# Cross-attention with two levels of Strassen products on one core: three sums of the next A move to the second stage, product 4's copied state changes its buffer, and a block's eviction changes its place

## The chip, the cores and the metric

The kernel runs on 1 core of one Trainium2 chip. The metric is the time of one execution in device microseconds (us); a kernel is run several times and the median is compared. The engines are TensorE (PE; its weight loads are a row of their own, PEld), VectorE (DVE), ScalarE (ACT), GpSimd (POOL) and SyncE (SP). SP, ACT and POOL also issue DMAs; those that POOL issues here with `accum_op` add the source to what lies in the destination.

## The reference

For each of 8 batches, with x1 and x2 of 512 x 1024 (channels x positions), in float32:

```python
q = jnp.einsum('bcn,dc->bnd', x1, Wq) + bq          # D = 64
k = jnp.einsum('bcn,dc->bdn', x2, Wk) + bk[:, None]
v = jnp.einsum('bcn,dc->bdn', x2, Wv) + bv[:, None]
attn = jax.nn.softmax(jnp.einsum('bnd,bdm->bnm', q, k), axis=2)
out = jnp.einsum('bcm,bnm->bcn', v, attn) + x1
```

## The kernel before

The kernel doesn't form v. It computes E, the exponentials of the scores with m on the partitions, then in a **first stage** Y = x2 E (512 x 1024, contracted over 1024 positions), whose columns are divided by the sums of E, and in a **second stage** O = Wv Y (contracted over 512 channels). Bias bv and x1 are added when O leaves PSUM.

Both stages are one 2 x 2 Strassen-Winograd step: seven products of blocks instead of eight. The left matrix (A, loaded as the transpose of x2; W in the second stage) gives four sums, the right one (E, then Y) four more:

```python
LEFT = (
    ("S1", "21", "22", ALU.add),
    ("S2", "S1", "11", ALU.subtract),
    ("S3", "11", "21", ALU.subtract),
    ("S4", "12", "S2", ALU.subtract),
)
```

The right sums T1 to T4 are built alike. `sum_a` makes the left sums of A on DVE (line 109, 128x1024 each; S3 overwrites block 21), `sum_e` and `sum_y` the right ones (line 254). `MULT` says which blocks product i multiplies and in which PSUM pair it accumulates: products 1, 6, 5, 3 run one after the other in the pair "a" (a0, a1), products 2, 7, 4 in the pair "c" (c0, c1; 2 by itself, 7 and 4 together). `multiply` issues a whole product (line 301: 16 matmuls in the first stage, 8 in the second), and after products 1, 6 and 5 ACT copies the running state of "a" to SBUF (line 312, tiles u1, u6, u5). These tiles become the place where a result block is put together: `evict_o` adds PSUM and bias to the tile on DVE (line 496), has POOL issue the accumulating DMA of x1 into it (line 499) and SP the store (line 500). Block 12 goes through ACT into a tile of tag "r" (line 492) instead. So block 11 of O is completed in u1, 22 in u5, 21 in u6.

From the second batch on, products 2, 3 and 4 of the first stage are themselves done with a Strassen step (the inner step): `inner_left` (line 333, four 128x256 operations) and `inner_right` (line 344, four 128x512) make its sums on DVE, `inner_product` its seven small products (line 351) with ACT copies between them (line 360). `multiply_2` is product 2; its two chains stand in c0 and c1, and its results are added on DVE (line 397). `multiply_onto` is product 3 (in "a") or 4 (in "c"): ACT copies go to a tile d and a tile v, and `complete` (line 422, DVE) adds v to d. The tags of d and v are arguments; a tile of a tag with one buffer can be written only when the readers of the tile before in that tag are done. Product 3 has its v in tag "r", product 4 in tag "u1", the tag of the tile that product 1 of the second stage copies to next.

`period(s, n, nn, nnn)` is one turn of the loop over the batches: the first and second stage of batch s, mixed with the scores, maxima and exponentials of the next batch n, the queries and keys of nn and a load for nnn. The program is scheduled by hand (`tc.manual_schedule()`): each engine executes its instructions in the order in which the program issues them, and waits at the head of its queue for what the instruction needs. So the place of a line in `period` is its place in the queue of its engine. Lines that will be spoken of:

- first stage, in order: products 1 and 2, `sum_t4`, S4, T3, product 6, scores of n for half 0 and queries of nn, maxima (`fold`, line 211; `highest`, line 215 and POOL's all-reduce, line 220), product 5, exponentials of n (lines 248 on DVE, 249 on ACT), `start_sum` (ACT line 507, then three accumulating DMAs from POOL, line 509), the right sums of product 3, `sum_a(n, "S1", "S2", "S3")`, product 7, `evict_y` of block 22 (line 462), product 3 with its eviction (lines 422, 442), the scaling of three blocks of Y (line 464), scores of n for half 1 (the third pair of scores stands in "a", its copies are line 197, the others' 199) and keys of nn, T1 and T2 of Y, maxima, `total` (line 215, POOL's all-reduce at line 225), product 4 (its sums at lines 422 and 432), block 21 of Y (lines 462, 464);
- second stage: products 1, 6, 2, 5, 7, 3, 4 on PE, with T3, T4, the exponentials of n for half 1 and the evictions of O on DVE between them, and the inner sums of product 2 of the next batch.

In the first batch (b = 0) there are no inner steps, and S1, S2 and S3 of the next A are made in the second stage already, with block 21 of O between them.

Of the kernel before, what the change touches and what calls it, by code (L numbers as in the profile page):

```python
# [15 lines left out]
def kernel(  # L16
# [117 lines left out]
    def sum_a(s, *ks):  # L134
        for k in ks:
            if k != "S3":
                s.a[k] = sb.tile([P, MH, C // 2], F32, tag=f"a{k}", name=f"a{k}_{s.b}")
        left_sums(s.a, *ks)
# [188 lines left out]
    def inner_left(s, i, x, tag):  # L327

        v = {f"{p + 1}{q + 1}": x[:, ts(q, MH // 2), ts(p, P)] for p in range(2) for q in range(2)}
        sums = sb.tile([P, 4, MH // 2, P], F32, tag=tag, name=f"aI{i}_{s.b}")  # L330
        for z, (k, x, y, op) in enumerate(LEFT):
            v[k] = sums[:, z]
            nc.vector.tensor_tensor(v[k], v[x], v[y], op)
        s.inner[i] = v
# [29 lines left out]
    def inner_bank(s, i, z):  # L364
        return ps_s.tile([P, 2, H], F32, tag="sc", name=f"ps_i{i}{z}_{s.b}")[:, 0, left]
# [35 lines left out]
    def multiply_onto(s, i, d_tag, v_tag):  # L401

        b0, b1 = (s.bank[MULT[i][2], j] for j in range(2))
        chain, third = inner_bank(s, i, 0), inner_bank(s, i, 2)
        d = sb.tile([P, 2, 2, H // 2], F32, tag=d_tag, name=f"d{i}_{s.b}")
        v = sb.tile([P, 2, H], F32, tag=v_tag, name=f"v{i}_{s.b}")[:, 0, left]
        for z, ps, opens, *copies in (
            (1, chain, True, d[:, 0, 0, :]),  # L410
            (7, third, True, v),
            (6, chain, False, d[:, 1, 0, :]),
            (2, b0[:, left], False),
            (5, chain, False, d[:, 0, 1, :], d[:, 1, 1, :]),
            (4, b1[:, left], False),
            (3, b0[:, right], False),
        ):
            inner_product(s, i, z, ps, opens, *copies)

        def complete():  # L420
            both = v.unsqueeze(1).to_broadcast([P, 2, H // 2])
            nc.vector.tensor_tensor(d[:, 1], d[:, 1], both, ALU.add)

        return d.rearrange("p j a n -> p j (a n)"), complete

    def multiply_4(s):

        d, complete = multiply_onto(s, 4, "u5", "u1")
        complete()
        for j in range(2):  # L430
            u6 = s.tmp[6][:, j, :]
            nc.vector.tensor_tensor(u6, u6, d[:, j, :], ALU.add)
# [33 lines left out]
    def evict_o(s, k):  # L466


        bank, add = RESULT[k]
        r, h = int(k[0]) - 1, int(k[1]) - 1  # L470

        def at(x):
            return x[s.b, 2 * r * P : 2 * (r + 1) * P, ts(h, H)].rearrange("(t p) n -> p t n", p=P)

        def bias(j):
            return bv_sb[:, 2 * r + j : 2 * r + j + 1]

        if s.b == B - 1:
            o = s.x[:, 2 * r : 2 * r + 2, ts(h, H)]
            for j in range(2):  # L480
                nc.vector.scalar_tensor_tensor(
                    o[:, j, :], s.bank[bank, j], bias(j), o[:, j, :], ALU.add, ALU.add
                )
            for j in range(2):
                if add is not None:
                    nc.vector.tensor_tensor(o[:, j, :], o[:, j, :], s.tmp[add][:, j, :], ALU.add)
                nc.sync.dma_start(out[s.b, ts(2 * r + j, P), ts(h, H)], o[:, j, :])
            return
        if add is None:
            o = sb.tile([P, 2, H], F32, tag="r", name=f"r_{s.b}")  # L490
            for j in range(2):
                nc.scalar.activation(o[:, j, :], s.bank[bank, j], AF.Identity, bias=bias(j))
        else:
            o = s.tmp[add]
            for j in range(2):
                nc.vector.scalar_tensor_tensor(  # L496
                    o[:, j, :], s.bank[bank, j], bias(j), o[:, j, :], ALU.add, ALU.add
                )
        nc.gpsimd.dma_start(o, at(x1), accum_op=ALU.add)  # L499
        nc.sync.dma_start(at(out), o)  # L500
# [107 lines left out]
    def period(s, n, nn, nnn):  # L608

        def first(i):
            multiply(s, "y", i, s.a, s.t, MH)

        def second(i):
            multiply(s, "o", i, w, s.y, 2)

        open_t(s)
        if n is None:
            load_x(s, x1)  # L620
        first(1)
        if s.b == 0:
            head_second(s, n)
        sum_e(s, "T1", "T2")
        if s.b == 0:
            total(s, 0)
        else:
            shares(s, 0)
        if n:
            load_a(n, "11")  # L630
        if s.b == 0:
            first(2)
            evict_y(s, "11", (1,))
            keys(n)
            load_x(nn, x1)
            sum_t4(s)
            sums(s, 1)
            shares(s, 0)
        else:
            evict = multiply_2(s)  # L640
            if s.b > 1:
                sums(s, 1)
            evict()
            sum_t4(s)
            sum_a(s, "S4")
            if s.b == 1:
                sums(s, 1)
        sum_e(s, "T3")
        if n:
            load_a(n, "21", "22")  # L650
        first(6)
        if s.b:
            inner_right(s, 4, s.t["T4"], "eT2")
            inner_left(s, 3, s.a["S4"], "aI3")

        def next_queries():
            queries(nn)
            load_x(nn, x2)

        def next_keys():  # L660
            keys(nn)
            if nnn:
                load_x(nnn, x1)

        if n:
            scores_and(n, 0, "c", next_queries if nn else nothing)
            for i in range(1, MH):
                fold(n, 0, i, "max", ALU.max)
            highest(n, 0)
        shares(s, 1)  # L670
        first(5)
        if n:
            for i in range(MH):
                exponentials(n, 0, i)
            start_sum(n, 0)
        if s.b:
            inner_right(s, 3, s.t["22"], "eT1")
            if n:
                sum_a(n, "S1", "S2", "S3")
        first(7)  # L680
        if s.b > 1:
            inner_left(s, 4, s.a["22"], "a12")
        if s.b:
            evict_y(s, "22", (1,))
            multiply_3(s)()
            for k in ("11", "12", "22"):
                evict_y(s, k, (2,))
        else:
            evict_y(s, "11", (2,))
            evict_y(s, "22")  # L690
            first(3)
            evict_y(s, "12", (1,))
        if s.b == 1:
            inner_left(s, 4, s.a["22"], "a12")
        if n:
            scores_and(n, 1, "a", next_keys if nn else nothing)
        sum_y(s, "T1")
        sum_y(s, "T2")
        if n:
            if s.b == 0:  # L700
                left_sums(w, "S1", "S2", "S3", "S4")
            for i in range(1, MH):
                fold(n, 1, i, "max", ALU.max)
            highest(n, 1)
            if s.b:
                total(n, 0)
        if s.b:
            multiply_4(s)
        else:
            first(4)  # L710
        if n:
            load_a(n, "12")
        evict_y(s, "21")
        second(1)
        sum_y(s, "T3")
        sum_y(s, "T4")
        second(6)
        if n:
            exponentials(n, 1, 0)
            exponentials(n, 1, 1)  # L720
        second(2)
        evict_o(s, "11")
        if s.b == 0:
            total(n, 0)
        second(5)
        if n:
            exponentials(n, 1, 2)
            exponentials(n, 1, 3)
        second(7)
        evict_o(s, "22")  # L730
        if n:
            if s.b:
                inner_left(n, 2, n.a["12"], "aS4")
            else:
                sum_a(n, "S1")
            second(3)
            evict_o(s, "12")
            if s.b:
                inner_right(n, 2, n.e[0][:, 1], "eT4")
            else:  # L740
                sum_a(n, "S2")
            second(4)
            evict_o(s, "21")
            if s.b == 0:
                sum_a(n, "S3")
                inner_left(n, 2, n.a["12"], "aS4")
                inner_right(n, 2, n.e[0][:, 1], "eT4")
        else:
            second(4)
            evict_o(s, "21")  # L750
            second(3)
            evict_o(s, "12")
# [37 lines left out]
```

## Time and profile before

| | |
|---|---|
| Time, median of 3 runs (lowest to highest) | 704.3 us (704.13 to 704.95) |
| Profiled execution: its own time | 704.53 us |
| Profiled execution: span from first to last instruction | 702.8 us |
| Granted TensorE clock over it | 0.999 |
| PE busy | 689.1 us, 2144 matmuls |
| DVE busy | 601.5 us, 730 instructions |
| ACT busy | 251.4 us, 390 instructions |
| POOL busy | 173.6 us, 135 instructions |
| Moved by DMA | 102.72 MB, mean 146 GB/s |

The table's durations are those of one profiled execution. A row of the timeline gives the start in us from the span's beginning, the duration, the engine, the line of the kernel, the operation, output and input, their shapes and how many instructions were merged; in brackets stands the idle time of the engine just before and what ended it. A row of the waits gives who waited for whom: us in total, how often, the longest. Periods of the loop are counted by their batch, 0 to 7; in the profile period 1 starts at 122.52 us, period 2 at 209.02, period 6 at 546.87 and period 7 at 629.05.

### The profile page before, as it was taken

To read this page: it belongs to the slowest core of one execution; us is meant where nothing else is said; L and a number is where in the kernel's file an instruction comes from. 1 tells how busy PE (TensorE), PEld (TensorE's weight loads), DVE (VectorE), ACT (ScalarE), POOL (GpSimd) and SP (SyncE) were. 2 spreads that over 40 slices of the span, in tenths; PEclk is the share of its full clock that TensorE was granted. 3 is DMA by queue.
4 is the path that set the end of the run, shared out by engine and by line. 5 is a ranking of instruction groups with operands and counts; after the bars stand their busy time and mean duration, and the time that the engine had idled before them with its cause. 6 is when DMAs were issued, how large, how long until landed. Compare 5 with 4: busy or idle time off the path is not lost.

```text
span 702.8 us, 6246 instructions
## 1 busy us (share of the span) xinstructions
PE 689.1 (98%) x2144; PEld 346.3 (49%) x2144; DVE 601.5 (86%) x730; ACT 251.4 (36%) x390; POOL 173.6 (25%) x135
## 2 busy tenths in 40 slices
PE   8999999999999999999999999999999999899997
PEld 4333444535545455454654556454554545545563
DVE  0998776989989899798998989889898889989584
ACT  2733424146231543225432344423444136232120
POOL 0124314132423123221142222222231222322000
PEclk9999999999999999999999999999999999999999
DMA  9666375864558454765639467285643824269003
GB/s 331 222 214 233 92 209 94 185 196 81 181 103 232 145 101 155 156 187 150 129 118 185 153 173 187 60 181 159 156 89 63 207 76 76 60 107 268 15 1 120
DMA packets 41248, 102.72 MB, mean 146 GB/s; under 512 B 4608, under 2 KB 4608, under 8 KB 41216
## 3 DMA queue, kind: packets, MB, share of 16 engines
q1 hardware_dynamic: 24256, 70.26, 29.3%
q0 software_dynamic: 15696, 29.96, 25.2%
q10 hardware_dynamic: 1264, 2.10, 0.9%
q8 instruction: 17, 0.28, 0.2%
q14 instruction: 15, 0.12, 0.1%
HBM read 72.62 MB, written 16.81 MB: 127 GB/s over the span
## 4 chain that ended last, share of the span: by engine, by line
PE 80%; DVE 12%; DMA 4%; issue 2%; ACT 1%; SPq 1%; POOL 1%; DVEq 0%; ACTq 0%
PE ps_ya L301 21%; PE ps_oa L301 14%; PE ps_oc L301 12%; PE ps_i L351 11%; PE ps_yc L301 7%; PE ps_s L190 5%; PE ps_q L148 3%; PE ps_k L148 3%; PE ps_ya L351 3%; DVE max L211 2%; PE ps_yc L351 2%; DMA a<-in_x2T_dram 1%; DMA x_in_x_dram<-in_x_dram 1%; DVE y L464 1%; DVE e L248 1%
## 5 line engine op out<-in xcount | busy, mean ns | idle before, releaser
L301 PE MATMUL ps_ya<-eT,aS 128*128 128x512 f32 x256 | 113.1, 595 | 0.0
L312 ACT COPY uy<-ps_ya 128x512 f32<-128x512 f32 x48 | 28.1, 588 | 163.7 <-PE ps_ya L301 157.4
L248 DVE TENSOR_TENSOR e<-e,top 128x1024 f32<-128x1024 f32 x60 | 72.0, 1251 | 15.5 <-POOL top L220 15.5
L301 PEld LDWEIGHTS ps_ya<-eT,aS 128*128 128x128 f32 x256 | 48.0, 190 | 60.9 <-issue 59.4
L249 ACT ACTIVATE e<-e 128x1024 f32<-128x1024 f32 x60 | 61.5, 1054 | 27.9 <-DVE e L248 26.4
L220 POOL PARTITION_ALL_REDUCE top<-max x16 | 32.4, 2026 | 146.2 <-DVE max L215 75.3
L301 PE MATMUL ps_yc<-e,a 128*128 128x512 f32 x144 | 63.4, 593 | 0.0
L225 POOL PARTITION_ALL_REDUCE den<-sum x16 | 56.0, 3497 | 22.8 <-DVE sum L215 17.8
L351 PE MATMUL ps_i<-eI,aI 128*128 128x256 f32 x252 | 60.4, 380 | 1.2 <-ACT sum L507 1.1
L301 PE MATMUL ps_oc<-y,w 128*128 128x512 f32 x128 | 57.7, 593 | 1.3 <-DVE y L464 1.3
L301 PE MATMUL ps_oa<-yT,w_S 128*128 128x512 f32 x128 | 57.6, 593 | 1.2 <-ACT uo L312 1.2
L301 PE MATMUL ps_ya<-e,a 128*128 128x512 f32 x128 | 56.3, 593 | 0.8 <-ACT e L243 0.8
L199 ACT COPY e<-ps_s 128x1024 f32<-128x1024 f32 x47 | 46.7, 1027 | 22.3 <-PE ps_s L190 21.3
L312 ACT COPY uo<-ps_oa 128x512 f32<-128x512 f32 x48 | 27.8, 586 | 74.9 <-PE ps_oa L301 60.5
L496 DVE SCALAR_TENSOR_TENSOR uo<-ps_oc,bv_sb,uo 128x512 f32<-128x512 f32 x42 | 30.9, 747 | 27.3 <-PE ps_oc L301 25.1
L351 PEld LDWEIGHTS ps_i<-eI,aI 128*128 128x128 f32 x252 | 47.2, 190 | 9.1 <-ACT sum L507 1.8
L499 POOL DMA_DIRECT2D uo<-in_x_dram x21 | 25.0, 1189 | 104.0 <-DVE uo L496 98.0
L254 DVE TENSOR_TENSOR eT<-e,eT 128x1024 f32<-128x1024 f32 x32 | 48.8, 1545 | 0.5
L190 PE MATMUL ps_s<-q,k 64*128 64x512 f32 x188 | 47.3, 608 | 1.6 <-ACT q L524 0.8
L509 POOL DMA_DIRECT2D sum<-e x21 | 25.3, 1205 | 78.2 <-DMA sum<-e 58.7
L301 PEld LDWEIGHTS ps_yc<-e,a 128*128 128x128 f32 x144 | 27.3, 190 | 34.8 <-issue 33.6
L211 DVE TENSOR_TENSOR max<-max,e 128x1024 f32<-128x1024 f32 x32 | 39.2, 1225 | 3.7 <-ACT e L197 0.5
(117 smaller groups left out, 1063.7 us busy)
## 6 DMA issues: line engine op xcount, KB each, us to landing
x_in_x_dram<-in_x_dram SPq DMA_DIRECT2D x60, 512.0 KB, 6.0
a<-in_x2T_dram SPq DMA_DIRECT2D x32, 512.0 KB, 6.7
sum<-e POOLq DMA_DIRECT2D x21, 512.0 KB, 5.0
uo<-in_x_dram POOLq DMA_DIRECT2D x21, 512.0 KB, 5.9
out_dram<-uo SPq DMA_DIRECT2D x21, 512.0 KB, 4.5
x_head<-in_x_dram SPq DMA_DIRECT2D x8, 512.0 KB, 8.2
den<-row POOLq DMA_DIRECT2D x16, 256.0 KB, 3.6
r<-in_x_dram POOLq DMA_DIRECT2D x7, 512.0 KB, 6.0
```

Source lines behind the costliest of these rows:

```text
L148: nc.tensor.matmul(ps[r, :], w_sb[:, c, :], s.x[:, c, ts(h, H)], start=(c == 0), stop=(c == CT - 1),)
L190: nc.tensor.matmul(ps[g], s.k[r, ts(i, P)], s.q[r, ts(h, H)], start=True, stop=True)
L199: nc.scalar.copy(e[:, :, i, :], whole)
L211: nc.vector.tensor_tensor(f, e[:, :, 0, :] if i == 1 else f, new, op)
L220: nc.gpsimd.partition_all_reduce(s.top[h], s.mx[h][:, 0, :], P, ReduceOp.max)
L225: nc.gpsimd.partition_all_reduce(s.den[h], s.mx[h][:, 0, :], P, ReduceOp.add)
L248: nc.vector.tensor_tensor(e, e, top, ALU.subtract)
L249: nc.scalar.activation(e, e, AF.Exp)
L254: nc.vector.tensor_tensor(t[k], t[x], t[y], ALU.subtract)
L301: nc.tensor.matmul(ps, left[ka][:, k, ts(j, P)], right[kb][:, k, :], start=opens and k == 0, stop=i in (2, 3, 4) and k == n_k - 1, skip_gr ...
L312: nc.scalar.copy(s.tmp[i][:, j, :], ps)
L351: nc.tensor.matmul(ps, s.inner[i][ka][:, k, :], s.inner[i, "t"][kb][:, k, :], start=opens and k == 0, stop=z in (2, 3, 4) and k == MH // 2 ...
```

## The change

Three edits, all in the order of instructions and in one tag:

1. From the second batch on, S1, S2 and S3 of the next A are no longer made in the first stage (between the right sums of product 3 and product 7), but in the second: S1 and S2 ahead of the eviction of block 22 of O, S3 behind it, ahead of the inner sums of product 2.
2. The copied state v of product 4 takes its tile from tag "r" instead of "u1".
3. In the first batch S1, S2, S3 and the inner sums of the next batch's product 2 all stand ahead of the eviction of block 21 of O, which becomes DVE's last step there. (In later batches block 21 was last before.)

```diff
     def multiply_4(s):
-        d, complete = multiply_onto(s, 4, "u5", "u1")
+        d, complete = multiply_onto(s, 4, "u5", "r")
...
         if s.b:
             inner_right(s, 3, s.t["22"], "eT1")
-            if n:
-                sum_a(n, "S1", "S2", "S3")
         first(7)
...
         second(7)
+        if s.b and n:
+            sum_a(n, "S1", "S2")
         evict_o(s, "22")
         if n:
-            if s.b:
-                inner_left(n, 2, n.a["12"], "aS4")
-            else:
-                sum_a(n, "S1")
+            if s.b == 0:
+                sum_a(n, "S1", "S2")
+            sum_a(n, "S3")
+            inner_left(n, 2, n.a["12"], "aS4")
+            inner_right(n, 2, n.e[0][:, 1], "eT4")
             second(3)
             evict_o(s, "12")
-            if s.b:
-                inner_right(n, 2, n.e[0][:, 1], "eT4")
-            else:
-                sum_a(n, "S2")
             second(4)
             evict_o(s, "21")
-            if s.b == 0:
-                sum_a(n, "S3")
-                inner_left(n, 2, n.a["12"], "aS4")
-                inner_right(n, 2, n.e[0][:, 1], "eT4")
```

The same instructions are issued as before; the queues of PE, POOL and SP and the order on ACT stay as they were.

## The prediction

> **What bounds the kernel now.** I read the page's busy row, then a table of windows with one row for each period of the loop (one batch and the preparation of the next), then the waits, then the timeline of VectorE (DVE) and TensorE (PE) around the places where PE stands still.
>
> ```profile
> PE 689.1 (98%) x2144; PEld 346.3 (49%) x2144; DVE 601.5 (86%) x730; ACT 251.4 (36%) x390; POOL 173.6 (25%) x135
> ...
> 122.52:209.02 86.50, 85.11 (x270) 43.31 (x269) 80.82 (x102) 32.08 (x50) 23.21 (x17) 1.00 0.60 148
> 209.02:293.48 84.46, 84.46 (x270) 43.56 (x269) 75.94 (x93) 31.99 (x50) 22.23 (x17) 1.00 0.61 154
> 293.48:377.94 84.46, 84.46 (x270) 43.56 (x269) 75.90 (x93) 31.98 (x50) 22.27 (x17) 1.00 0.60 153
> ...
> 546.87:629.05 82.18, 78.57 (x237) 41.09 (x237) 75.85 (x93) 29.93 (x47) 22.24 (x17) 1.00 0.44 100
> ```
>
> After the length of the window come the busy times of PE, PEld and DVE. Periods 2 to 5 (four, each 84.46 or 84.47 us) have PE busy from end to end: nothing done to DVE can shorten them. Period 1 takes 86.50, so 2.04 us too much. Period 6 has no projections for a batch after next: two of 3.58 us less, so it should take 84.46 - 7.16 = 77.30; it takes 82.18, 4.9 us too much. With DVE at 75.85 of them, DVE is nearly the bound there. So at most about 6.9 us can be won in the periods whose order changes. The waits say by whom:
>
> ```profile
> PE ps_sa L190 <- DVE y L442: 1.4, 1, 1.4
> PE ps_oc L301 <- DVE y L464: 1.3, 2, 0.8
> PE ps_oa L301 <- ACT uo L312: 1.2, 1, 1.2
> PE ps_i L351 <- ACT sum L507: 1.1, 2, 0.9
> ...
> ACT uo L312 <- DVE d L422: 8.3, 2, 5.0
> ```
>
> Period 6, DVE first, then PE:
>
> ```profile
> 585.61 1.22 DVE L109 TENSOR_TENSOR aS<-a,a 128x1024 f32<-128x1024 f32 x1
> 586.87 1.22 DVE L109 TENSOR_TENSOR aS<-aS,a 128x1024 f32<-128x1024 f32 x1
> 588.01 1.22 DVE L109 TENSOR_TENSOR a<-a,a 128x1024 f32<-128x1024 f32 x1
> 589.14 0.42 DVE L333 TENSOR_TENSOR aI<-a 128x256 f32<-128x256 f32 x1
> ...
> 593.94 1.13 PE L190 MATMUL ps_sa<-q,k 64*128 64x512 f32 x4 [1.36 <-DVE y L442]
> ...
> 607.18 3.70 PE L301 MATMUL ps_oa<-yT,w_S 128*128 128x512 f32 x8 [1.16 <-ACT uo L312]
> 611.65 3.67 PE L301 MATMUL ps_oc<-y,w 128*128 128x512 f32 x8 [0.77 <-DVE y L464]
> ```
>
> The first three rows are S1, S2, S3 of the next A. Everything behind them on DVE's queue, down to block 21 of Y (L464), which product 2 of the second stage needs at 611.65, is late by what they take.
>
> **The change part by part.** The two orders hold the same instructions; TensorE's, SP's and POOL's queues and DMAs are the same. Only DVE's order and one buffer change.
>
> *1. S1 to S3 leave the first stage (periods 1 to 6).* They take 589.14 - 585.61 = 3.53 us of queue. What is late next is no longer DVE: L422 needs ACT's last copy of product 3, L442 its last group on PE. In the undisturbed period 2 these come 1.74 us after that product's group 5 starts (253.24; L422 at 254.98 after an idle of 0.68 for ACT) and 0.82 after its group 3 starts (254.96; L442 at 255.78).
> - Periods 2 to 5: DVE already waited for ACT there. The 3.5 us become waiting: 0.
> - Period 6: group 3 starts at 589.63, so L442 moves from 592.60 to 590.45, 2.15 earlier. Its wait of 1.36 at ps_sa goes (PE gets there at 590.59 + 1.82 = 592.41, L442 is through at 591.7). ACT's copies of the scores are late next: 3.86 us from first to last as in period 1 (171.73 to 175.59), so until 595.63, and product 4 waits some 0.4. PE, 1.46 earlier by then, could start product 2 at 602.43 - 1.46 + 2 x 3.43 = 607.83. From L442 to product 2 DVE takes 611.65 - 592.60 = 19.05, so it starts at 590.45 + 19.05 = 609.50 instead of 611.65: gain 2.15, DVE still the bound.
> - Period 1: group 3 at 169.59 gives L442 at 170.41 instead of 171.09; product 2 at 190.94 instead of 191.62, where PE is ready at about 190.9: gain 0.7. The other 1.05 lost there (PE waits for ACT's sum L507 at 165.20) lies before the moved work and stays.
>
> *2. They come into the second stage.* Period 2's tail, by its own rows:
>
> ```profile
> 281.07 2.34 DVE L248 TENSOR_TENSOR e<-e,top 128x1024 f32<-128x1024 f32 x2
> 285.01 0.75 DVE L496 SCALAR_TENSOR_TENSOR uo<-ps_oc,bv_sb,uo 128x512 f32<-128x512 f32 x1 [1.59 <-PE ps_oc L301]
> 286.72 0.75 DVE L496 SCALAR_TENSOR_TENSOR uo<-ps_oc,bv_sb,uo 128x512 f32<-128x512 f32 x1 [0.96 <-PE ps_oc L301]
> ...
> 291.80 0.75 DVE L496 SCALAR_TENSOR_TENSOR uo<-ps_oc,bv_sb,uo 128x512 f32<-128x512 f32 x1 [0.34 <-PE ps_oc L301]
> 293.52 0.75 DVE L496 SCALAR_TENSOR_TENSOR uo<-ps_oc,bv_sb,uo 128x512 f32<-128x512 f32 x1 [0.97 <-PE ps_oc L301]
> ```
>
> S1 and S2 (2.40) fit into 1.59 + 0.96 of idle: from 283.34 to 285.74, block 22 at 285.74 and, as before, 286.72. S3 (1.14), the inner sums (1.47 and 2.55) then run to about 292.55; block 21 leaves at 292.55 and, as before, 293.52. Zero lag. Behind these evictions wait product 4 (289.9, bank c) and, in the next period, product 2's inner chains in the same bank, 6.87 us after its start: both have over 2 us of slack. In periods 1 and 6 DVE comes later relative to PE (idle only 0.35 before block 22), and ends 0.7 to 0.8 late; the next period's DVE then meets an idle of 0.74 (it waits for ACT's copies at L397), which takes that up. If the cover goes, lag beyond 0.74 passes on to the row maximum, but PE feels it only after a further 2.3 us, by which ACT waits for PE at product 3's first copy. So 0 now, PE time only beyond 3.0 us of lag.
>
> A rule against this: the Trainium skill, SBUF — State Buffer, Who interferes with whom, says that a VectorE instruction with two SBUF inputs and a GpSimd instruction that reads SBUF exclude each other, the second blocking fully. All-reduces run beside L422 and L432 in period 6: 1.53 + 3.33 us there, 0.69 + 1.29 in period 7 without them, 2.88 more. By the row this excess moves along with DVE, since DVE's own maxima and sums release the all-reduces. By the rule, were the issue order to flip, the second L432 would run after the last all-reduce (ends 610.15, plus 0.68, against 609.63): 1.2 us more, period 6 gaining 0.95, the total 1.65. I take the row: periods 1, 2 and 6 all show 3.33.
>
> *3. Product 4's copied state in tag "r".* The two 128x512 copies of product 1 (ACT L312) no longer wait for L422 (5.0 us in period 6), and PE's 1.16 at product 6 goes. But y21 is late behind it, so the wait moves to product 2: 0 on its own. Tag "r" is free: product 3's state is read by 590.3, product 4's is written after 596, block 12 comes 20 us later.
>
> *4. Period 0: block 21 last on DVE.* S3 and the inner sums fill idle of 1.94 + 0.97; block 21 leaves until 125.3 instead of 123.23, and DVE starts T1 about 3 us earlier. But L397 at 134.15 waits for ACT's copy (11.79 after the first product's start, exactly as in period 2): the lead is lost there, gain 0. Cost: block 21's accumulate and store start up to 2.1 later, and ACT's copy of the next product 6 already waits for that store until 140.44. Its second copy is due at 142.34, so up to 1.9 is free; behind it wait four score copies, whose PSUM banks PE needs from 144.91. Bounds: no gain, 0 to 0.3 lost; I take 0, because the accumulate queues behind block 12's anyway (10.3 us to landing).
>
> Sum: 2.15 + 0.7 = 2.85 us. The profiled execution took 704.53 (span 702.8); it would take 701.7. The median shown is 704.3, 0.23 lower: 701.4.
>
> **The rivals.**
> *A, the freed time meets another wait.* In period 6 the sum (L215) needs the third accumulate, issued at 596.57; L215 would be due at 602.18. Landings of 5.0 to 5.8 put it at 601.6 to 602.4. Uncovered, the queue behind it, y21 included, waits. At 7.3 to landing period 6 gains 0.45; with period 1's 0.7 and the price of part 4 the total is about 1.0: 703.3, no change. Likewise with the flipped lock. For it: a margin of 0.6 at the usual 5.0. Against: from 597 to 602 the trace shows no other transfer.
> *B, slower.* The moved sums stretch to double in their new place, beside POOL's issue of block 22's accumulate. Then 3.5 us of lag come in six periods; beyond 3.0, 0.5 to 1.0 us of PE each time, 3 to 6 in all, and periods 1 and 6 keep nothing: 708. It decides at 3.0 us of lag. Against it: aI and eI keep 0.42 and 0.69 right beside that issue (287.77, 1.18 us).
> *C, the change does less than it says:* the buffer is not the product's own but shared with product 3's state and block 12; if one of them were late, ACT would wait as before, which costs nothing while y21 is the bound. Its time is that of the forecast.
>
> **How the numbers follow.** Forecast (with C) 0.80: 701.4, its own range 700.6 to 702.8 (0.8 below for offsets read from other periods, 1.4 above for the same and the lock's 1.2). A 0.12: 703.3. B 0.08: 708. This kernel's time can tell about 0.2%, 1.4 us, from no change. Faster 0.80, same 0.12, slower 0.08. The range goes from 700.6 to 703.9, taking in A and leaving out B.
>
> **What would show it.** Right: windows of periods 2 to 5 unchanged at 84.46, period 6 near 80.0, period 1 near 85.8; no PE wait at ps_sa; ACT's wait for L422 gone; PE's wait at product 2 of period 6 grown to about 1.7, on L464. DVE idle of some 3.5 us before L422 in periods 2 to 5, and next to none before block 22. Wrong: any of the four steady periods longer, S1 to S3 above 1.3 us in their new place, PE waiting for scores in period 1, or L215 waiting for a DMA in period 6.

## The result, and the profile after

The changed kernel takes 701.41 us (median of 5 runs, 701.05 to 701.9) against 704.57 (5 runs, 704.13 to 704.95) on the same chip: ratio 0.9956, 95% interval 0.9942 to 0.9971. A second measurement on another occasion gave 701.31 against 704.24, ratio 0.9958 (0.9946 to 0.9971). The forecast was 701.4. The profiled execution of this kernel took 701.41 us, its span 699.6.

First the page's busy row of the changed kernel, and behind it the windows of periods 1, 2, 3, 6 and 7 (length; busy PE, PEld, DVE, ACT, POOL with counts; granted clock; DMA share; GB/s):

```profile
PE 688.7 (98%) x2144; PEld 346.8 (50%) x2144; DVE 598.7 (86%) x730; ACT 251.4 (36%) x390; POOL 173.7 (25%) x135
...
122.16:207.97 85.81, 84.92 (x270) 43.39 (x269) 77.10 (x97) 32.15 (x50) 23.21 (x17) 1.00 0.58 149
207.97:292.43 84.46, 84.46 (x270) 43.56 (x269) 76.36 (x95) 31.98 (x50) 22.23 (x17) 1.00 0.63 155
292.43:376.89 84.46, 84.46 (x270) 43.56 (x269) 75.22 (x93) 31.98 (x50) 22.27 (x17) 1.00 0.59 153
...
545.81:625.93 80.12, 78.04 (x238) 41.26 (x237) 75.05 (x93) 29.90 (x47) 22.23 (x17) 1.00 0.45 104
625.93:699.60 73.67, 69.64 (x205) 38.42 (x203) 53.86 (x76) 12.05 (x26) 7.29 (x7) 1.00 0.37 103
```

Measured between the first matmuls of product 1, period 1 goes from 86.50 to 85.81 us (0.69 less), periods 2 to 5 take 337.84 both times, and period 6 goes from 82.19 to 80.12 (2.07 less). Period 7 differs by 0.08. The remaining 0.36 us of the spans' 3.2 lies ahead of period 1: before, PE waits twice for 0.2 us on the first loads of x, and among the eleven profiles with the new order of period 0 the start of period 1 lies anywhere from 121.81 to 122.67 us. It is not counted as the change's. So the agreement of 701.41 with the forecast 701.4 to the last digit is in part luck: 0.36 us of the distance did not come from the change.

The rows of the waits that answer to those shown of before:

```profile
PE ps_oc L301 <- DVE y L464: 1.5, 1, 1.5
PE ps_i L351 <- ACT sum L507: 1.1, 2, 0.9
PE ps_i L351 <- ACT e L199: 0.3, 1, 0.3
...
DVE d L422 <- ACT d L360: 26.2, 11, 4.2
```

PE's waits at `ps_sa` for L442 and at `ps_oa` for ACT's copy are gone, and so is ACT's wait for L422. What is left of them stands in one place, product 2 of period 6. The last row is where the time that DVE won in the other periods lies: before L422 it now waits for ACT 11 times, 26.2 us in all, against 9 times and 8.1 us before. Period 6 of the changed kernel, DVE and then PE:

```profile
588.68 0.69 DVE L422 TENSOR_TENSOR d<-d,v 128x512 f32<-128x512 f32 x1 [1.29 <-ACT d L360]
589.47 1.29 DVE L442 TENSOR_TENSOR y<-ps_ya,d 128x512 f32<-128x512 f32 x2
601.21 0.68 DVE L215 TENSOR_TENSOR sum<-sum 128x512 f32<-128x512 f32 x1
603.26 3.33 DVE L432 TENSOR_TENSOR uy<-uy,d 128x512 f32<-128x512 f32 x2
617.04 1.21 DVE L109 TENSOR_TENSOR aS<-a,a 128x1024 f32<-128x1024 f32 x1
618.29 1.23 DVE L109 TENSOR_TENSOR aS<-aS,a 128x1024 f32<-128x1024 f32 x1
620.75 1.22 DVE L109 TENSOR_TENSOR a<-a,a 128x1024 f32<-128x1024 f32 x1
...
594.67 1.99 PE L351 MATMUL ps_i<-eI,aI 128*128 128x256 f32 x8 [0.29 <-ACT e L199]
608.53 3.67 PE L301 MATMUL ps_oc<-y,w 128*128 128x512 f32 x8 [1.55 <-DVE y L464]
```

The rows of L442 and L432 before:

```profile
592.60 1.29 DVE L442 TENSOR_TENSOR y<-ps_ya,d 128x512 f32<-128x512 f32 x2
606.38 3.33 DVE L432 TENSOR_TENSOR uy<-uy,d 128x512 f32<-128x512 f32 x2
```

L422 now waits for ACT, as in the undisturbed periods: the 3.53 us of S1 to S3 no longer stand ahead of it. From L442 to product 2 it is 608.53 - 589.47 = 19.06 us; the prediction took 19.05 from before. L215 starts without idle time, so the third accumulating DMA came in time. L432 still shows 3.33 us for two operations. The last three DVE rows are S1, S2 and S3 in their new place, as long as they were before.

### The profile page after: what moved, and what is told of

It reads as the page before. It is cut to its first block, busy times and chain, and to the rows that moved or that the text cites. A ratio compares the mean times of both kernels' runs of the same rounds, so it can differ in the third digit from the quotient of the medians.

```text
span 699.6 us, 6250 instructions
## 1 busy us (share of the span) xinstructions
PE 688.7 (98%) x2144; PEld 346.8 (50%) x2144; DVE 598.7 (86%) x730; ACT 251.4 (36%) x390; POOL 173.7 (25%) x135
## 4 chain that ended last, share of the span: by engine, by line
PE 86%; DVE 10%; issue 1%; ACT 1%; DMA 1%; POOL 1%; DVEq 0%; ACTq 0%
PE ps_ya L301 21%; PE ps_oa L301 15%; PE ps_i L351 12%; PE ps_oc L301 12%; PE ps_yc L301 8%; PE ps_s L190 5%; PE ps_k L148 4%; PE ps_q L148 3%; PE ps_ya L351 2%; PE ps_yc L351 2%; DVE max L211 2%; DVE e L248 1%; DVE eT L254 1%; DVE e L254 1%; PE ps_sa L190 1%
## 5 line engine op out<-in xcount | busy, mean ns | idle before, releaser
L301 PEld LDWEIGHTS ps_oc<-y,w 128*128 128x128 f32 x128 | 24.1, 190 | 32.8 <-issue 30.6
```

The lines of the kernel that those rows point to most:

```text
L301: nc.tensor.matmul(ps, left[ka][:, k, ts(j, P)], right[kb][:, k, :], start=opens and k == 0, stop=i in (2, 3, 4) and k == n_k - 1, skip_gr ...
```

## The experiments

All kernels of this section were timed against the kernel before on the same chip. Lengths of periods are taken from the profiled execution, as above.

### 1. Each edit by itself

**The moved sums alone**: buffer and first batch as before.

```diff
             inner_right(s, 3, s.t["22"], "eT1")
-            if n:
-                sum_a(n, "S1", "S2", "S3")
...
         second(7)
+        if s.b and n:
+            sum_a(n, "S1", "S2")
         evict_o(s, "22")
         if n:
             if s.b:
+                sum_a(n, "S3")
                 inner_left(n, 2, n.a["12"], "aS4")
```

> Only S1 to S3 of the next A move to the second stage (batches 1 to 7 as n of periods 1 to 6); product 4's state stays in tag u1 and period 0 keeps its old order. Theory (DVE's queue between product 3 and block 21 of Y sets the start of product 2 in periods 1 and 6): the whole gain, 2.8 us against the kernel before; ACT still waits for L422 in period 6 and PE waits about 1.0 at product 6, but product 2 starts when it does in the changed kernel. Rival (the buffer is a cause of its own): only about 1.7 us are won, the 1.16 us of product 6 stay.

Measured: 701.11 us (700.78 to 701.67) against 704.15; ratio 0.9957 (0.9944 to 0.9969). Period 1 takes 85.79, period 6 79.62. The whole gain is this edit's. PE's waits in period 6:

```profile
603.77 3.70 PE L301 MATMUL ps_oa<-yT,w_S 128*128 128x512 f32 x8 [0.50 <-ACT uo L312]
608.24 3.67 PE L301 MATMUL ps_oc<-y,w 128*128 128x512 f32 x8 [0.77 <-DVE y L464]
```

With the old buffer the wait is split, 0.50 at product 6 for ACT's copy and 0.77 at product 2; with the new one (above) it stands whole at product 2, 1.55. The 0.50 was expected as about 1.0. From product 4's second group to product 2 it is 13.85 us here and 13.86 in the changed kernel, so the buffer moves the wait and gains nothing; the 0.5 us by which period 6 is shorter here lies ahead of it (last section).

**The buffer alone** (`multiply_onto(s, 4, "u5", "u1")` becomes `multiply_onto(s, 4, "u5", "r")`, nothing else).

> Only product 4's copied state moves from tag u1 to r. Theory: no change, under 0.1 us; in period 6 PE's wait of 1.16 at product 6 goes and its wait of 0.77 at product 2 grows to about 1.9. Rival (a cause of its own): 1.2 us faster.

Measured: 705.6 us (703.51 to 706.4), ratio 1.0013 (1.0003 to 1.0023): no gain. In the profiled execution (704.06 us) period 6 takes 82.17, as before, and the wait moved as the prediction said:

```profile
611.19 3.67 PE L301 MATMUL ps_oc<-y,w 128*128 128x512 f32 x8 [2.19 <-DVE y L464]
```

Before, it was 1.16 at product 6 and 0.77 at product 2. Six of the eleven runs lie at 705.6 to 706.4 with a granted clock of 0.998, the others at 703.5 to 704.4 with 0.999 or 1.0. The profile is of one of the faster ones, so what the slower ones met stays open. A candidate is the clock: in this profile PE's 2.19 us without work left it at 1.00, but 2.43 us in the last kernel of experiment 3 were enough to lower it, at a price of about 1.7 us. A buffer that gathers two stalls into one would then come near that point. No run here shows that it did.

**The first batch alone** (edit 3 of the change and no other).

> Only period 0 has the new order (block 21 last on DVE). Theory: no change; DVE reaches L397 of period 1 about 3 us earlier and waits there for ACT; product 2 of period 1 starts when it did. Rival (the earlier start of period 1 is worth something): up to 1.5 us faster. Rival (the later store holds up ACT): up to 0.3 us slower.

Measured: 703.87 us (703.54 to 704.84), ratio 0.9999 (0.999 to 1.0008): nothing, in either direction. DVE comes earlier and waits at L397:

```profile
133.87 0.69 DVE L397 TENSOR_TENSOR uy<-uy,i 128x512 f32<-128x512 f32 x1 [2.50 <-ACT i L360]
```

### 2. Do the steady periods pay or gain, and how much lag do they bear?

**The sums moved in periods 1 and 6 only**: the changed kernel, but periods 2 to 5 make S1 to S3 in the first stage as before.

```diff
             inner_right(s, 3, s.t["22"], "eT1")
+            if s.b not in (1, 6) and n:
+                sum_a(n, "S1", "S2", "S3")
...
-        if s.b and n:
+        if s.b in (1, 6) and n:
             sum_a(n, "S1", "S2")
...
-            sum_a(n, "S3")
+            if s.b in (0, 1, 6):
+                sum_a(n, "S3")
```

> The changed kernel, but periods 2 to 5 make S1 to S3 in the first stage as before; only periods 1 and 6 make them in the second. Theory: as fast as the changed kernel, 2.9 us faster than before, since periods 2 to 5 are bound by PE in either order (84.46 us each). Rival (the move costs or gains something in each period): a difference to the changed kernel of more than 0.5 us.

Measured: 701.19 us (701.06 to 702.06), ratio 0.9961 (0.9948 to 0.9973). Periods 1 and 6 take 85.80 and 80.12, periods 2 to 5 84.46 each. The gain is made in two of the six periods, and four of them neither pay nor gain.

**More sums in the new place**: the changed kernel, with S2 of the next A computed two (then four) more times on DVE ahead of block 21 of O in periods 2, 3 and 4. The result is the same; 1.2 us of DVE are added each time.

```diff
             inner_right(n, 2, n.e[0][:, 1], "eT4")
+            if s.b in (2, 3, 4):
+                for _ in range(2):
+                    nc.vector.tensor_tensor(n.a["S2"], n.a["S1"], n.a["11"], ALU.subtract)
```

> The changed kernel with two more 128x1024 additions on DVE ahead of block 21 of O in periods 2, 3 and 4 (S2 of the next A made over again, with the same result): 2.4 us, some 2.0 us of lag behind PE at the end of the period. Theory (lag is covered up to 3.0 us: 0.74 before L397 and 2.3 before ACT's first copy of product 3): as fast as the changed kernel within 0.3 us, periods 3 to 5 stay at 84.46 us. Rival (no such cover, each us of lag costs PE): 1.5 to 2 us in each of periods 3 to 5, some 5 us.

> The same with four more additions: 4.75 us, some 4.3 us of lag. Theory (the cover ends at 3.0 us): periods 3, 4 and 5 take 1 to 1.6 us longer each, with PE waiting for ACT's sum or DVE's inner sums at product 3; 3 to 5 us slower than the changed kernel. Rival (no cover): 4 us in each, some 12 us slower. Rival (more cover than thought): no change.

Two more: 703.0 us (700.68 to 706.01), ratio 0.9986 (0.9972 to 1.0). The added work makes DVE begin its first instruction behind block 21 (T1, line 254) 2.04 us later relative to PE than in the kernel before, and the periods behind it are unchanged; here periods 3 and 4 of the profiled execution (702.54 us):

```profile
292.25:376.71 84.46, 84.46 (x269) 43.56 (x269) 77.08 (x96) 31.96 (x50) 22.42 (x17) 1.00 0.60 153
376.71:461.17 84.46, 84.46 (x270) 43.56 (x269) 77.09 (x96) 31.97 (x50) 22.39 (x17) 1.00 0.61 153
```

What became longer is period 7, where nothing was added (75.05 us against 73.83):

```profile
634.95 0.37 ACT L360 COPY i<-ps_i 128x256 f32<-128x256 f32 x1 [1.65 <-DMA out_dram<-uo]
```

This is the first copied state of product 2, a tile of tag "u5", in which block 22 of the batch before was put together: the copy must wait until that block's store has read it. No step of the prediction names that wait. The store was issued at 628.3 and landed 6.6 us later. In the profiles of the changed kernel it landed 0.3 us (701.41 us) and 0.7 us (701.67 us) ahead of that copy.

Four more: 705.07 us (703.64 to 705.8), ratio 1.0012 (1.0003 to 1.0021), by the ratios some 3.8 us more than the changed kernel. Periods 3, 4 and 5, then DVE's wait and PE's in period 3, and one more of PE in period 4:

```profile
292.49:378.68 86.19, 84.70 (x270) 43.44 (x269) 78.03 (x98) 32.14 (x50) 22.16 (x17) 1.00 0.58 148
378.68:464.98 86.30, 84.87 (x270) 43.39 (x269) 81.66 (x99) 32.29 (x50) 21.87 (x17) 1.00 0.58 151
464.98:549.44 84.46, 84.46 (x269) 43.51 (x269) 79.33 (x98) 32.29 (x50) 22.38 (x17) 1.00 0.53 127
```

```profile
354.79 0.69 DVE L215 TENSOR_TENSOR sum<-sum 128x512 f32<-128x512 f32 x1 [3.73 <-DMA sum<-e]
361.28 3.67 PE L301 MATMUL ps_oc<-y,w 128*128 128x512 f32 x8 [1.49 <-DVE y L464]
...
402.67 1.13 PE L190 MATMUL ps_s<-q,k 64*128 64x512 f32 x4 [1.43 <-ACT e L199]
```

The forecast was 1 to 1.6 us in each of three periods, with PE waiting for ACT's sum or DVE's inner sums at product 3. It came otherwise: 1.7 and 1.8 us in two periods and nothing in the third, and none of the waits is the one forecast. Measured when DVE begins T1, the lag is 4.56 us in period 3, 5.47 in period 4 and 4.57 in period 5, so the same lag costs 1.7 in one and nothing in another. What differs is the traffic. In period 3 the third accumulate, issued at 345.75, lands after 9.0 us instead of 5.0, while SP has four 512 KB loads of x under way (issued from 346.72 on); L215 waits 3.73 us for it, and block 21 of Y comes late behind it. In period 5 there is no batch left to load x for; the accumulates land in 5.0 to 5.6, and nobody waits. That is the wait of rival A, met under a larger lag and with another transfer beside it. In period 4 the accumulate is late by 0.24 only; there ACT's copies of the scores wait 2.52 us for DVE's T4 (line 254), and PE waits for these copies.

### 3. What limits period 6 now

In the changed kernel `total` of half 0 (line 215 and POOL's all-reduce) stands ahead of product 4's sums on DVE, and these two L432 take 3.33 us there instead of 1.29. If `total` follows block 21 of Y, they should be short.

```diff
-            if s.b:
-                total(n, 0)
...
         evict_y(s, "21")
+        if n and s.b:
+            total(n, 0)
```

> The changed kernel, but from period 1 on the last sum of E's half 0 (L215) with its all-reduce (L225) comes behind block 21 of Y instead of ahead of product 4's sums. Theory (in period 6 DVE, slowed by the all-reduce beside L432, is the bound of product 2): L432 falls from 1.66 to about 0.65 us each, PE's wait of 1.55 at product 2 of period 6 goes, and about 0.15 in period 1: 1.7 us faster than the changed kernel, 699.7. Rival (something else is due just behind): under 0.7 us.

Measured: 704.82 us (699.78 to 706.74), ratio 1.0001 (0.9987 to 1.0014). In the profiled execution (705.04 us) period 6 takes 78.67, so 1.45 less (1.55 was expected), and product 2 starts without a wait. L432 did not become as short as told: 2.13 us for the two instead of 1.29, since the all-reduce of the maximum still runs beside it. The moved all-reduce now meets T4 of Y (line 254), which takes 3.26 us instead of 1.21. All of it and more is lost in period 7 (79.2 instead of 73.83). ACT, PE, then the windows around the stall:

```profile
635.79 0.37 ACT L360 COPY i<-ps_i 128x256 f32<-128x256 f32 x1 [4.04 <-DMA out_dram<-uo]
...
636.22 4.50 PE L351 MATMUL ps_i<-eI,aI 128*128 128x256 f32 x12 [3.36 <-ACT i L360]
...
630.00:636.00 6.00, 2.85 (x11) 1.71 (x9) 5.82 (x7) 0.80 (x2) 0.59 (x1) 1.00 0.93 257
636.00:640.00 4.00, 3.79 (x11) 3.15 (x12) 0.85 (x2) 0.91 (x3) 1.51 (x2) 0.66 0.92 245
```

It is the same wait for the same store, 4.04 us, and PE stands still for 3.36. Then the granted clock is 0.66 over 4 us and twelve matmuls take 4.50 us instead of 2.75.

**That tile in a tag of its own.** If the store is the cause, product 2's copied state must be free of it:

```diff
-        uv = sb.tile([P, 4, H // 2], F32, tag="u5", name=f"i26_{s.b}")
+        uv = sb.tile([P, 4, H // 2], F32, tag="i26", name=f"i26_{s.b}")
```

Four kernels were timed beside each other: the changed kernel again, and the edit on it, on the kernel with two more sums, and on the one with `total` later.

> The changed kernel once more, beside the three that follow. If the slow runs of the kernel with two more additions come from the store of block 22 of O (tile u5, which ACT's first copy of the next product 2 overwrites) and that store is on the edge in the changed kernel too: a spread upward by 1 to 4 us in some runs, above the 701.05 to 701.9 seen so far. Rival (the spread belongs to the added work alone): 701.0 to 702.

> The changed kernel with the copied states of product 2 in a tile of their own instead of tag u5. Theory (in period 7 ACT's first copy of product 2 waits in some runs for the store of block 22): at most 702 in every run, median 701.0 to 701.4. Rival (the spread is something else): as the changed kernel beside it, spread included.

> The kernel with two more additions in periods 2 to 4, with the copied states of product 2 in a tile of their own. Theory: 701.0 to 701.5 in every run, since periods 3 to 5 cover the lag and period 7 no longer waits for the store. Rival (the added work itself makes the slow runs): still 702 to 706 in most.

> The kernel with the later total, with the copied states of product 2 in a tile of their own. Theory: its period 7 no longer waits for the store (3.4 us of PE idle and the lowered clock behind it go), period 7 takes 73.7 instead of 79.2, and what period 6 won (1.45) is kept: 699.6 median, every run under 700.8. Rival (period 7 waits for something else of DVE's lag): 700.5 or more.

| kernel | us, median (range) | ratio to before (95%) |
|---|---|---|
| changed kernel again | 701.31 (701.17 to 701.8) | 0.9958 (0.9946 to 0.9971) |
| with the tile of its own | 701.21 (701.01 to 701.98) | 0.9959 (0.9945 to 0.9972) |
| two more sums, with it | 701.31 (701.18 to 701.78) | 0.9957 (0.9945 to 0.997) |
| `total` later, with it | 700.2 (699.77 to 700.38) | 0.9939 (0.9927 to 0.9952) |

With its own tile the kernel with two more sums takes what the changed kernel takes: 2.4 us of added DVE work in three periods cost nothing, and the spread of 5.3 us went with the shared tile. With `total` later the loss in period 7 is gone:

```profile
632.49 0.37 ACT L360 COPY i<-ps_i 128x256 f32<-128x256 f32 x1 [0.28 <-PE ps_i L351]
```

At 700.2 us this kernel is 1.1 us faster than the changed one; the forecast was 699.6, and every run under 700.8, which held. On the changed kernel itself the edit shows nothing, and no run of it went above 701.9, so the spread forecast for it did not come: in its two profiles the store lands in time, by 0.3 and 0.7 us. Why the kernel with two more sums in periods 2 to 4 misses by 1.4 us in period 7, whose instructions and order are those of the changed kernel, stays open.

**`start_sum` of half 0 later as well** (behind product 3's multiplication instead of behind product 5's exponentials, from the second batch on; product 2's state still in tag "u5"), so that fewer waits stand ahead of product 3:

```diff
-            start_sum(n, 0)
+            if s.b == 0:
+                start_sum(n, 0)
...
+            if n:
+                start_sum(n, 0)
```

> As the kernel before this one, and in addition, from period 1 on, ACT's copy that opens the sum (L507) comes behind product 3's copies instead of ahead of them. Theory: PE's wait for ACT's sum at product 3 goes, 1.05 us in period 1 and 0.2 to 0.3 in period 6: 1.2 us faster than the kernel with the later total alone, 698.5. Rival (the accumulating DMAs, started about 4.4 us later, hold up POOL's maximum or the total): no gain or a loss.

Measured: 724.15 us (723.33 to 724.67), ratio 1.0283 (1.0269 to 1.0296). Periods 1 to 4 take 88.75 to 90.0. In period 2 the sum comes late, then PE:

```profile
280.74 0.69 DVE L215 TENSOR_TENSOR sum<-sum 128x512 f32<-128x512 f32 x1 [3.59 <-DMA sum<-e]
288.74 5.40 PE L301 MATMUL ps_oc<-y,w 128*128 128x512 f32 x8 [2.44 <-DVE uo L496]
```

The third accumulate was issued at 270.80 and DVE went on at 280.74, so it took 9.9 us, and 9.4 to 9.9 in periods 1 to 4. Each time four 512 KB loads of x were under way, here issued from 266.36 on. The exponentials and the evictions of O queue behind L215, PE waits 2.44 us for a PSUM bank, and the product behind that wait takes 5.40 us instead of 3.60, at a lowered clock:

```profile
286.30:288.70 2.40, 0.00 (x0) 0.00 (x0) 2.40 (x4) 1.71 (x2) 0.26 (x1) 1.00 0.05 1
288.70:292.00 3.30, 3.26 (x5) 1.47 (x6) 3.30 (x4) 2.79 (x5) 1.20 (x1) 0.60 0.12 4
292.00:294.20 2.20, 2.20 (x5) 0.92 (x5) 2.17 (x3) 0.70 (x1) 0.00 (x0) 0.83 1.02 184
```

So the late accumulates decide, as the rival said, but in this kernel only where they meet the loads of x: period 5 has the same order and no such loads, its last two accumulates land in 5.0 and 5.5 us, L215 does not wait, and the period takes 84.46. Period 7 takes 78.4 instead of 73.83 by the store of block 22 again (ACT waits 3.2 us, PE 2.55). And the wait that was to go did not: in period 1 PE stands still for 0.89 us at product 3 as before, now for DVE's inner sums (line 344), which had been due together with ACT's sum.

## Why the prediction was right

- **S1 to S3 out of the first stage, period 6** (forecast 2.15): 2.07. The steps held singly: the wait at `ps_sa` went, product 4 waits 0.29 for ACT's score copies (forecast some 0.4), L442 to product 2 is 19.06 (19.05), and PE's wait there grew from 0.77 to 1.55 (some 1.7). DVE is still the bound. That the number came so close is in part luck: period 6 scatters by 0.5 us with what DVE loses beside an all-reduce, and the two profiles compared happen to be hit alike (2.12 and 2.20 us). The experiment with the sums alone shows that this edit carries the whole gain.
- **Period 1** (0.7): 0.69. Its 0.9 at ACT's sum L507 stayed.
- **Periods 2 to 5** (nothing): 84.46 each, with the sums in either place.
- **Into the second stage** (a lag of 0.8 at most, absorbed): S1 to S3 keep 1.21 to 1.23 us beside the evictions, so rival B's stretch did not come, and DVE starts periods 2 and 7 with 0.55 and 0.56 us of lag. The price told for more lag was wrong, though the change never came near it: the "3.0 us" of cover is no fixed size. A lag of 4.57 us was free in period 5, one of 4.56 cost 1.7 in period 3. What fails there is not ACT's first copy of product 3 but the sum L215, whose accumulate meets the loads of x, and in period 4 ACT's score copies. That the price forecast for two of the periods came out near is luck.
- **The lock between DVE and POOL** (the row of 2.88 us, not the rule's 1.2 more, from the Trainium skill, SBUF — State Buffer, Who interferes with whom): L432 is 3.33 again and product 2 came when the row said.
- **The buffer** (0 by itself): the wait went to product 2 whole, 2.19 there. The median of the buffer alone was 1.45 us higher, from runs whose cause is open; with the sums moved, the kernel with the old buffer (701.11) and the one with the new (701.41) have overlapping ranges, so no gain or loss of the buffer is shown there.
- **Period 0** (0, 0 to 0.3 lost): nothing alone. DVE's lead was lost at L397 as told. But the term "accumulate and store start up to 2.1 later" was right only for the accumulate: counted from the first matmul of period 1, block 21's accumulate is issued 2.05 later (125.30, 3.30 behind it, instead of 123.61, 1.25 behind it), and its store goes out 1.05 *earlier* (132.53 instead of 133.94). In the order of before, block 12's store and this accumulate run together and take 7.8 to 8.1 and 9.4 to 10.3 us in three profiles; in the new order they take 2.7 and 6.3 to 7.2. ACT's wait until 140.44, from which the prediction took its bound, belongs to that one execution: with the sums alone and with the buffer alone, where period 0 has its old order, the copy is released by PE, as it is after the change (138.54).
- **Sum**: 2.85 forecast; the two periods gave 2.76. The medians of the two measurements differ by 3.2 and 2.9 us, and 2.85 lies within the intervals of both.

What the prediction did not see: the store of block 22 behind product 2's copied state. In the changed kernel it costs nothing, but with 0.3 and 0.7 us to spare it stands so close that three of the experiments met it, and one more edit of the same kind (experiment 3) was worth nothing until that tile was moved.

## What to carry to other kernels

Removing work from an engine's queue is worth, in each period, only the distance to the wait that comes next: here 3.53 us less on DVE's queue gave 0, 0.7 and 2.1, and each was read beforehand from the rows behind the place, period by period. Moving it was free here because its new place had idle time and the readers behind it had slack. How much slack there is depends on the transfers under way too: a late accumulate cost nothing in the period without loads and 4 to 5 us in those with them. So for each tile behind the new place one should ask who writes it next, and whether a store still reads it then. When a shortening is followed by no gain, the next period's first waits are the place to look: a tile shared with a store took back all of the 1.45 us won in period 6, and with a tag of its own 1.1 us remained in the median.

## What the runs showed of the hardware that was not expected

- **A stall of PE costs more than its length.** After 3.36 us without matmuls the granted clock was 0.66 over the next 4 us (0.50 for 2 of them), and 12 matmuls took 4.50 instead of 2.75 us, so 1.75 more. After 2.44 us it was 0.60 over the next 3.3 us, and 8 matmuls took 5.40 instead of 3.60. All six waits of 2.43 to 3.36 us in the profiles were followed by such a fall, at 1.7 to 1.8 us each. After the only one of 2.19 us (with the buffer alone) it stayed at 1.00. The Trainium skill, TensorE: Matmul & The Clock Gate, Part 1: The HAM clock gate, tells of a gate that halves the clock after an idle window of about 3.4 us; the fall to 0.50 agrees, but here shorter idleness was enough, so the measured 2.43 us decides. In the kernels before and after no wait of PE in the loop is over 1.6 us.
- **What an all-reduce takes from DVE moves by half a microsecond between executions, and period 6 with it.** In period 6 the pair of T4 sums that meets POOL's all-reduce takes 4.47 us before, 4.55 after, 4.00 with the sums alone and 4.09 with the first batch alone, 2.35 where no all-reduce runs. In other executions it is an instruction ahead of the pair that is hit:

```profile
558.05 2.82 DVE L397 TENSOR_TENSOR uy<-uy,i 128x512 f32<-128x512 f32 x1 [0.74 <-ACT i L360]
```

```profile
558.83 2.65 DVE L397 TENSOR_TENSOR y<-i,uy 128x256 f32<-128x256 f32 x1
```

  (with the buffer alone, and with the sums moved in periods 1 and 6 only; 0.69 and 0.42 otherwise.) DVE loses 1.65 to 2.23 us in these six, whichever instruction it has under way, and less than the 3.2 us of the all-reduce, so the full blocking of the rule does not show over its whole length. The two profiles of the changed kernel differ in this too: in the second one line 397 is hit, 2.75 us instead of 0.42. Period 6 follows the loss: with the sums moved it takes 79.6 us at 1.65, 79.7 at 1.8 and 80.1 to 80.2 at 2.2 to 2.3; with the sums in the old place 81.8 at 1.74 and 82.2 at 2.12 and 2.13.
- **How long an accumulating DMA takes depends on what else is under way.** One of 512 KB landed in 5.0 to 5.2 us with no other large transfer beside it (period 6 before), in 9.4 to 9.9 us beside the four loads of x (`start_sum` later), and in 9.4 to 10.3 beside a store issued behind it (period 0 before). So one that is issued 2.05 us later, together with that store, landed earlier. An all-reduce that POOL issues right behind it is not the reason: in period 5 of the kernel with `start_sum` later it follows at the same distance of 0.74 us as in period 2, and the last one lands within 5.5.
